# Moving the output projection of a time-mix block behind its FFN, and two early splits of W1

## The chip, the core and the metric

The kernel runs on one core of one Trainium2 chip. The metric is the time of one execution on the device, in microseconds. Before the change it is 949.51 us, the median of three runs (948.9 to 949.73). The profiled execution has a span of 947.2 us, and all clock times below are counted from the start of that span.

## What is computed

Input x is [4, 1024, 512] in f32. It is layer-normalised, and two branches start from the normalised rows.

```
xn  = layernorm(x)
xx  = previous row of xn (row 1 for row 0) - xn
k   = (xn + xx * time_mix_k) @ Wk.T          # 704 hidden channels
r   = (xn + xx * time_mix_r) @ Wr.T
state[t] = state[t-1] * exp(-exp(decay)) + relu(k[t])
att = layernorm((state * r) @ Wv.T) * gamma + beta
ffn = f16(gelu(f16(xn) @ W0.T + bias0) as f16 @ W1.T + bias1)     # 2048 channels
out = x + att + ffn
```

The products of the first branch are taken in f32. For the FFN the weights are split into a high and a low part of type f32r, and each is multiplied with an f16 value held as f32r, so a product of the FFN is two matmuls.

## The kernel before the change

The rows are cut into 8 blocks of 512 tokens, and each block has four subtiles of 128 tokens. The program is unrolled. A scheduler turns the written order into one instruction order for each engine; it uses its own estimates, and it may pull an operation that is written later ahead of others where it believes an engine to be idle. [...]

A block goes through these stages on TensorE, in this order:

- `attention` (line 289). The 704 hidden channels are five chunks of 128 and a half chunk of 64. For each full chunk four matmuls make `pk` and four make `pr` (line 313). ScalarE takes relu of `pk` into `rk` (line 298), VectorE runs the recurrence over it (`st`, line 300) and multiplies by `pr` into `g` (line 324). For the half chunk, k and r share one accumulator, `pkr`: k goes to its partitions 0 to 63 and r to 64 to 127 (lines 328 and 329), and the results go to `gh` (line 336).
- `ffn` (line 398). It is a loop over 16 chunks of the 2048 channels. `up(n)` is eight matmuls into `pd` (line 408), a gelu on ScalarE (line 416) and a cast to f32r on VectorE into `d` (line 418). `down(n, s)` is two matmuls into `pe[s]` for each of the four subtiles (line 423). Two `up` stand ahead of the first `down`.
- `attention_out` (line 341) is called from within that loop, at n = 0. That places the output projection `po` behind pd of chunks 0 and 1. It is 20 full matmuls (line 348, the contraction over 128 channels) and 4 with 64 contraction rows (line 358). `residual` (line 362) then normalises each `po` on VectorE (lines 178, 369, 372, 373) and adds x.
- At n = 4 and n = 7 the loop prepares the next block: layernorm, 16 stream transposes into `xnT` (line 199) and the mixes (lines 276 and 278).
- `finish` (line 391) rounds `pe` to f16 and adds it into the output rows.

PSUM is two pools of four banks: `ps_mm` for pk, pr, pkr, pd and po, and `ps_e` for pe (and for the transposes of block 0). Buffers are taken in turn, so a matmul that opens an accumulator waits for the reader of the accumulator four places earlier.

In block 0 the weights are also prepared. `load_w0(g)` (line 128) loads a quarter of W0 in four pieces and splits each: a copy on ScalarE (line 119) and a subtraction on VectorE (line 120). `load_w1(0, n)` (line 135) does the same with one chunk of W1 and writes both parts to DRAM (line 149), from where later blocks read them (line 151). The raw pieces of W0 and W1 share three buffers, `raw`, so a load waits for the subtraction that ends the use of the buffer.

Of the kernel before, what the change touches and what calls it, by code (L numbers as in the profile page):

```python
# [8 lines left out]
F16 = mybir.dt.float16  # L9
F32 = mybir.dt.float32  # L10
# [4 lines left out]
P = 128  # L15
# [4 lines left out]
def time_mix_and_gelu_ffn(  # L20
# [26 lines left out]
    nc = tc.nc  # L47
    B, T, C = x.shape
    HID = wkT.shape[1]
    N = w0T.shape[1]  # L50
    TB = 512
# [237 lines left out]
    def attention(i, xk):  # L289


        b, t0 = blocks[i]
        g = one.tile([P, NF, TB], F32, tag="g", name=f"g_{i}")
        gh = one.tile([P, NS // 2, P], F32, tag="gh", name=f"gh_{i}")

        def states(h, hw, pk):
            rk = two.tile([P, TB], F32, tag="rk", name=f"rk_{i}_{h}", bufs=1)
            nc.scalar.activation(rk[:hw], pk, AF.Relu)  # L298
            st = two.tile([P, TB], F32, tag="st", name=f"st_{i}_{h}")
            nc.vector.tensor_tensor_scan(  # L300
                st[:hw],
                w_sb[:hw, h : h + 1].to_broadcast([hw, TB]),
                rk[:hw],
                0.0 if t0 == 0 else carry[:hw, h : h + 1],
                ALU.mult,
                ALU.add,
            )
            if t0 + TB < T:
                nc.gpsimd.tensor_copy(carry[:hw, h : h + 1], st[:hw, TB - 1 : TB])
            return st  # L310

        def product(dst, w, cols, src, c):
            nc.tensor.matmul(dst, w[c][:, cols], src, start=(c == 0), stop=(c == NC - 1))  # L313

        for h in range(NF):
            cols = slice(h * P, (h + 1) * P)
            pk = ps_mm.tile([P, TB], F32, tag="mm", name=f"pk_{i}_{h}")
            for c in range(NC):
                product(pk, wk_sb, cols, xk[:, c, :], c)
            st = states(h, P, pk)  # L320
            pr = ps_mm.tile([P, TB], F32, tag="mm", name=f"pr_{i}_{h}")
            for c in range(NC):
                product(pr, wr_sb, cols, xnT[:, c, 1:], c)
            nc.vector.tensor_mul(g[:, h, :], st, pr)  # L324

        both = ps_mm.tile([P, TB], F32, tag="mm", name=f"pkr_{i}")
        for c in range(NC):
            product(both[:HF], wk_sb, slice(H0, HID), xk[:, c, :], c)
            product(both[HF:], wr_sb, slice(H0, HID), xnT[:, c, 1:], c)
        st = states(NF, HF, both[:HF])  # L330

        def tokens(ap, odd):
            return ap.rearrange("p (s two t) -> p s two t", two=2, t=P)[:, :, odd, :]

        for odd in range(2):
            nc.vector.tensor_mul(
                gh[odd * HF : (odd + 1) * HF], tokens(st[:HF], odd), tokens(both[HF:], odd)
            )
        return g, gh

    def attention_out(i, g, gh):

        b, t0 = blocks[i]
        pos = [ps_mm.tile([P, C], F32, tag="mm", name=f"po_{i}_{s}") for s in range(NS)]

        def full(s, first):
            for h in range(NF):
                nc.tensor.matmul(  # L348
                    pos[s],
                    g[:, h, s * P : (s + 1) * P],  # L350
                    wv_sb[:, h, :],
                    start=(first and h == 0),
                    stop=(not first and h == NF - 1),
                )

        def half(s, first):
            rows = slice(s % 2 * HF, (s % 2 + 1) * HF)
            nc.tensor.matmul(  # L358
                pos[s], gh[rows, s // 2, :], wv_sb[rows, NF, :], start=first, stop=not first
            )  # L360

        def residual(s):
            xr = two.tile([P, C], F32, tag="xres", name=f"xres_{i}_{s}")
            nc.sync.dma_start(xr, x[b, t0 + s * P : t0 + (s + 1) * P, :])
            mv = four.tile([P, 1, 2], F32, tag="mv1", name=f"mvy_{i}_{s}")
            stats_of(mv, 0, pos[s], f"sty_{i}_{s}")
            rstd = rstd_of(mv[:, :, 1], f"ry_{i}_{s}")
            z = four.tile([P, C], F32, tag="z", name=f"z_{i}_{s}")
            nc.vector.scalar_tensor_tensor(
                z, pos[s], mv[:, 0, 0:1], gamma_sb, ALU.subtract, ALU.mult  # L370
            )
            nc.vector.scalar_tensor_tensor(z, z, rstd, beta_sb, ALU.mult, ALU.add)
            nc.vector.tensor_add(z, z, xr)
            return z

        early, late = range(NS // 2), range(NS // 2, NS)
        for s in early:
            full(s, True)  # L380
        for s in early:
            half(s, False)
        for s in late:
            half(s, True)
        zs = [residual(s) for s in early]
        for s in late:
            full(s, False)
        zs += [residual(s) for s in late]
        return zs

    def finish(i, s, z, pe):
        b, t0 = blocks[i]
        e16 = two.tile([P, C], F16, tag="e16", name=f"e16_{i}_{s}")
        nc.vector.tensor_add(e16, pe, b1_sb)  # L394
        nc.vector.tensor_add(z, z, e16)  # L395
        nc.sync.dma_start(out[b, t0 + s * P : t0 + (s + 1) * P, :], z)

    def ffn(i, xf, between, state):


        pe = [ps_e.tile([P, C], F32, tag="pe", name=f"pe_{i}_{s}") for s in range(NS)]

        def up(n):
            pd = ps_mm.tile([P, TB], F32, tag="mm", name=f"pd_{i}_{n}")
            cols = slice(n * P, (n + 1) * P)
            for c in range(NC):
                for w in (w0h, w0l):
                    nc.tensor.matmul(  # L408
                        pd,
                        w[c][:, cols],  # L410
                        xf[:, c, :],
                        start=(c == 0 and w is w0h),
                        stop=(c == NC - 1 and w is w0l),
                    )
            d16 = two.tile([P, TB], F16, tag="d16", name=f"d16_{i}_{n}")
            nc.scalar.activation(d16, pd, AF.Gelu, bias=b0_sb[:, n : n + 1])  # L416
            d = wide.tile([P, TB], F32R, tag="d", name=f"d_{i}_{n}", bufs=4)
            nc.vector.tensor_copy(d, d16)  # L418
            return d

        def down(n, s, d, w1):
            for part in range(2):
                nc.tensor.matmul(  # L423
                    pe[s],
                    d[:, s * P : (s + 1) * P],
                    w1[part],
                    start=(n == 0 and part == 0),
                    stop=(n == NN - 1 and part == 1),
                )

        last = 3 if i == len(blocks) - 1 else 0
        AHEAD = 2
        waiting = [(up(n), load_w1(i, n)) for n in range(AHEAD)]
        for n in range(NN):
            if n in between:
                between[n]()
            if n + AHEAD < NN:
                waiting.append((up(n + AHEAD), load_w1(i, n + AHEAD)))  # L440
            if n < NN - last:
                operands = waiting.pop(0)
                for s in range(NS):
                    down(n, s, *operands)
        if last:
            with tc.manual_schedule(engines={nc.tensor.engine, nc.vector.engine}):
                for s in range(NS):
                    for n, operands in zip(range(NN - last, NN), waiting):
                        down(n, s, *operands)
                    finish(i, s, state["zs"][s], pe[s])  # L450
        return pe

    behind = ExitStack()
# [2 lines left out]
    nc.scalar.activation(w_sb, w_sb, AF.Exp)  # L456
    nc.scalar.activation(w_sb, w_sb, AF.Exp, scale=-1.0)
    xf = ffn_input(0, x16s)
    for i in range(len(blocks)):
        more = i + 1 < len(blocks)  # L460
        state = {}
        gs = attention(i, xk)
        if i == 0:
            for grp in range(N // W0G):
                load_w0(grp)
            behind.close()
            load_late_constants()
# [1 line left out]
            x_now = load_x(i + 1)  # L469

        def out_stage():
            state["zs"] = attention_out(i, *gs)

        def next_norm():
            layernorm(i + 1, x_now)
# [2 lines left out]
            transposed(x_now)  # L478
            state["mixed"] = mixed_inputs(i + 1)

        between = {0: out_stage}
        if more:
            between[4] = next_norm
            between[7] = next_inputs
        pe = ffn(i, xf, between, state)
        if more:
            x16s, xk = state["mixed"]
            xf = ffn_input(i + 1, x16s)
            for s in range(NS):
                finish(i, s, state["zs"][s], pe[s])  # L490


# [41 lines left out]
```

## Time and profile before

| What | Value |
|---|---|
| Time, median of 3 | 949.51 us |
| Span of the profiled run, granted TensorE clock | 947.2 us, 0.997 |
| PE busy | 931.0 us (98%) |
| VectorE busy | 485.7 us (51%) |
| ScalarE busy | 160.5 us (17%) |
| pd and pe matmuls (lines 408, 423), records | 1024 and 1024 |
| pk, pr, full po matmuls (lines 313, 348), records | 320 each |
| pkr and half po matmuls, records | 128 and 64 |
| Moved from and to HBM | 89.14 and 16.78 MB |

The page puts 98% of the span on TensorE, but matmul ends are modelled, so lengths below are taken as distances between starts. An f32 matmul appears as two records. In the chain of waits every row is a stretch of the work that ended last; "x8" counts records.

### The profile page before, as it was taken

How to read it: one execution, taken by the hardware profiler on the slowest of the kernel's cores; microseconds unless marked ns; L12 is line 12 of the kernel's file. 1: busy time of each engine (PE TensorE's matmuls, PEld its weight loads, DVE VectorE, ACT ScalarE, POOL GpSimd, SP SyncE). 2: the span in 40 equal slices, each digit the busy share in tenths (PEclk: the TensorE clock that was granted, in tenths of full speed). 3: DMA queues.
4: the chain of work that ended last, by engine and by line, in shares of the span. 5: the costliest groups of instructions: out<-in, count | busy, mean ns of one | idle time of the engine just before them, and what ended most of it. 6: DMA issues, size and time to landing. Idle time of an engine off the chain costs nothing.

```text
span 947.2 us, 8658 instructions
## 1 busy us (share of the span) xinstructions
PE 931.0 (98%) x3216; PEld 583.0 (62%) x3216; DVE 485.7 (51%) x836; ACT 160.5 (17%) x264; POOL 53.7 (6%) x128
## 2 busy tenths in 40 slices
PE   5999999999999999999999999999999999999998
PEld 2447764478644785448854488545884458744686
DVE  6558852385424844259443593436924269232513
ACT  5322321012100121002201022010210102111021
POOL 1011000010001000011000100001000020000100
PEclk9999999999999999999999999999999999999999
DMA  8734570045400354004540155301542024410243
GB/s 271 240 133 145 209 268 1 0 134 199 157 0 21 136 186 148 0 24 142 190 134 1 33 165 180 111 1 57 184 161 88 0 80 143 160 62 0 69 153 111
DMA packets 43368, 106.47 MB, mean 112 GB/s; under 512 B 8256, under 2 KB 8256, under 8 KB 43328
## 3 DMA queue, kind: packets, MB, share of 16 engines
q1 hardware_dynamic: 43328, 105.94, 33.4%
q8 instruction: 25, 0.41, 0.2%
q14 instruction: 15, 0.12, 0.0%
HBM read 89.14 MB, written 16.78 MB: 112 GB/s over the span
## 4 chain that ended last, share of the span: by engine, by line
PE 93%; DVE 4%; ACT 1%; issue 1%; DMA 0%; POOL 0%; DVEq 0%
PE pd L408 23%; PE pe L423 22%; PE po L348 15%; PE pr L313 15%; PE pk L313 14%; PE pkr L313 3%; PE po L358 2%; DVE xnT L199 1%; DVE w L120 1%; DVE stx L178 0%; DVE d L418 0%; DMA x<-in_L_attn_x 0%; DVE z L395 0%; DVE e L394 0%; DVE xk L278 0%
## 5 line engine op out<-in xcount | busy, mean ns | idle before, releaser
L423 PE MATMUL pe<-w,d 128*128 128x512 f32 x1024 | 251.2, 390 | 1.4 <-DVE w L120 0.8
L423 PEld LDWEIGHTS pe<-w,d 128*128 128x128 f32 x1024 | 192.2, 188 | 42.4 <-DVE d L418 1.5
L408 PE MATMUL pd<-xf,w0h 128*128 128x512 f32 x512 | 203.8, 398 | 0.0
L408 PE MATMUL pd<-xf,w0l 128*128 128x512 f32 x512 | 199.9, 390 | 0.0
L416 ACT ACTIVATE d<-pd,b_sb 128x512 f16<-128x512 f32 x128 | 87.9, 686 | 418.2 <-PE pd L408 399.2
L313 PE MATMUL pk<-xk,wk 128*128 128x512 f32 x320 | 145.9, 599 | 3.1 <-DVE xk L245 3.1
L313 PE MATMUL pr<-xnT,wr 128*128 128x512 f32 x320 | 144.0, 592 | 0.0
L348 PE MATMUL po<-wv_sb,g 128*128 128x512 f32 x320 | 140.8, 595 | 0.0
L418 DVE CAST d<-d 128x512 fp32r<-128x512 f16 x128 | 54.1, 424 | 130.7 <-ACT d L416 129.7
L408 PEld LDWEIGHTS pd<-xf,w0h 128*128 128x128 f32 x512 | 96.2, 188 | 28.0 <-issue 5.7
L408 PEld LDWEIGHTS pd<-xf,w0l 128*128 128x128 f32 x512 | 96.2, 188 | 21.6 <-issue 1.9
L313 PEld LDWEIGHTS pk<-xk,wk 128*128 128x128 f32 x320 | 61.0, 192 | 78.3 <-issue 70.9
L313 PEld LDWEIGHTS pr<-xnT,wr 128*128 128x128 f32 x320 | 60.7, 190 | 76.8 <-issue 76.1
L348 PEld LDWEIGHTS po<-wv_sb,g 128*128 128x128 f32 x320 | 60.2, 190 | 75.5 <-issue 74.8
L199 DVE STREAM_TRANSPOSE xnT<-x 32x512 f32<-32x512 f32 x112 | 78.7, 703 | 2.2
L300 DVE TENSOR_TENSOR_SCAN st<-w_sb,carry,rk 128x512 f32<-128x512 f32 (+1 forms) x24 | 30.8, 1282 | 70.2 <-ACT rk L298 70.2
L298 ACT ACTIVATE rk<-pk 128x512 f32<-128x512 f32 x40 | 24.0, 600 | 232.9 <-PE pk L313 232.9
L178 DVE BATCH_NORM_STATS2 sty<-po 128x6 f32<-128x512 f32 x32 | 22.1, 690 | 73.4 <-PE po L358 67.9
L300 DVE TENSOR_TENSOR_SCAN st<-w_sb,rk 128x512 f32<-128x512 f32 (+1 forms) x24 | 29.3, 1222 | 53.6 <-ACT rk L298 53.5
L324 DVE TENSOR_TENSOR g<-st,pr 128x512 f32<-128x512 f32 x40 | 27.5, 688 | 53.7 <-PE pr L313 53.6
L172 POOL TENSOR_SCALAR ry<-mvy 128x1 f32<-128x1 f32 x32 | 11.4, 357 | 503.4 <-DVE mvy L179 503.4
L313 PE MATMUL pkr<-xnT,wr 128*64 128x512 f32 x64 | 29.2, 598 | 0.0
(56 smaller groups left out, 439.6 us busy)
## 6 DMA issues: line engine op xcount, KB each, us to landing
w<-w1d SPq DMA_DIRECT2D x111, 512.0 KB, 3.2
x<-in_L_attn_x SPq DMA_DIRECT2D x32, 256.0 KB, 3.4
xres<-in_L_attn_x SPq DMA_DIRECT2D x32, 256.0 KB, 2.7
w1d<-w SPq DMA_DIRECT2D x16, 512.0 KB, 3.0
out<-z SPq DMA_DIRECT2D x32, 256.0 KB, 4.8
w0raw<-in_L_ffn_W SPq DMA_DIRECT2D x16, 256.0 KB, 4.5
w1raw<-in_L_ffn_W SPq DMA_DIRECT2D x16, 256.0 KB, 3.5
wk<-in_L_attn_Wk SPq DMA_DIRECT2D x4, 352.0 KB, 6.0
```

The source lines that it names most:

```text
L178: nc.vector.bn_stats(st6, src)
L199: nc.vector.transpose(dst[i * Q : (i + 1) * Q, :, :, j, :], src[j * Q : (j + 1) * Q, :, :, i, :],)
L298: nc.scalar.activation(rk[:hw], pk, AF.Relu)
L300: nc.vector.tensor_tensor_scan(st[:hw], w_sb[:hw, h : h + 1].to_broadcast([hw, TB]), rk[:hw], 0.0 if t0 == 0 else carry[:hw, h : h + 1], A ...
L313: nc.tensor.matmul(dst, w[c][:, cols], src, start=(c == 0), stop=(c == NC - 1))
L324: nc.vector.tensor_mul(g[:, h, :], st, pr)
L348: nc.tensor.matmul(pos[s], g[:, h, s * P : (s + 1) * P], wv_sb[:, h, :], start=(first and h == 0), stop=(not first and h == NF - 1),)
L358: nc.tensor.matmul(pos[s], gh[rows, s // 2, :], wv_sb[rows, NF, :], start=first, stop=not first)
L408: nc.tensor.matmul(pd, w[c][:, cols], xf[:, c, :], start=(c == 0 and w is w0h), stop=(c == NC - 1 and w is w0l),)
L416: nc.scalar.activation(d16, pd, AF.Gelu, bias=b0_sb[:, n : n + 1])
L418: nc.vector.tensor_copy(d, d16)
L423: nc.tensor.matmul(pe[s], d[:, s * P : (s + 1) * P], w1[part], start=(n == 0 and part == 0), stop=(n == NN - 1 and part == 1),)
```

## The change

Three things change.

- The output projection of blocks 0 to 6 leaves the FFN loop. `attention_out(i)` now runs behind the FFN of block i. Amid it, between the four half matmuls of `po` and the last ten full ones, the half chunk of k and r of block i+1 is computed (`half_chunk`); then the rest of po, and then the five full chunks of block i+1 (`full_chunks`). The last block keeps its projection inside its FFN. The half chunk's accumulator `pkr` moves from `ps_mm` to `ps_e`.
- `finish` is cut in two. `rounded` makes the f16 rows `e16` right after the FFN, which frees `pe`; the buffers for `e16` go from two to four.
- In block 0 the chunks 0 and 1 of W1 are loaded and split behind the first quarter of W0 and ahead of the other three, since the first `down` no longer has the projection of block 0 in front of it.

The core of the diff:

```diff
-        for h in range(NF):
...
-        both = ps_mm.tile([P, TB], F32, tag="mm", name=f"pkr_{i}")
...
+        def full_chunks():
+            g = one.tile([P, NF, TB], F32, tag="g", name=f"g_{i}")
...
+        def half_chunk():
+            gh = one.tile([P, NS // 2, P], F32, tag="gh", name=f"gh_{i}")
+            both = ps_e.tile([P, TB], F32, tag="pe", name=f"pkr_{i}")
...
         for s in late:
             half(s, True)
+        amid()
         zs = [residual(s) for s in early]
...
-        e16 = two.tile([P, C], F16, tag="e16", name=f"e16_{i}_{s}")
+        e16 = four.tile([P, C], F16, tag="e16", name=f"e16_{i}_{s}")
...
         if i == 0:
-            for grp in range(N // W0G):
+            load_w0(0)
+            early = [load_w1(0, n) for n in range(2)]
+            for grp in range(1, N // W0G):
                 load_w0(grp)
...
-        between = {0: out_stage}
-        if more:
-            between[4] = next_norm
-            between[7] = next_inputs
-        pe = ffn(i, xf, between, state)
+        pe = ffn(i, xf, {4: next_norm, 7: next_inputs} if more else {0: out_stage}, state, early)
...
+            e16s = [rounded(i, s, pe[s]) for s in range(NS)]
             xf = ffn_input(i + 1, x16s)
+            full_chunks, half_chunk = attention(i + 1, xk)
+            next_gh = []
+            zs = attention_out(i, g, gh, lambda: next_gh.append(half_chunk()))
+            gh = next_gh[0]
             for s in range(NS):
-                finish(i, s, state["zs"][s], pe[s])
+                finish(i, s, zs[s], e16s[s])
+            g = full_chunks()
```

More of the change, by code (lines that the diff above doesn't have):

```diff
@@ L292, in attention @@
         b, t0 = blocks[i]
-        g = one.tile([P, NF, TB], F32, tag="g", name=f"g_{i}")
-        gh = one.tile([P, NS // 2, P], F32, tag="gh", name=f"gh_{i}")
         def states(h, hw, pk):
@@ L313, in product @@
             nc.tensor.matmul(dst, w[c][:, cols], src, start=(c == 0), stop=(c == NC - 1))
-        for h in range(NF):
[L316 to L324, printed above, removed]
@@ L326, in attention @@
-        both = ps_mm.tile([P, TB], F32, tag="mm", name=f"pkr_{i}")
[L327 to L330, printed above, removed]
+        def full_chunks():
+            g = one.tile([P, NF, TB], F32, tag="g", name=f"g_{i}")
+            for h in range(NF):
+                cols = slice(h * P, (h + 1) * P)
+                pk = ps_mm.tile([P, TB], F32, tag="mm", name=f"pk_{i}_{h}")
+                for c in range(NC):
+                    product(pk, wk_sb, cols, xk[:, c, :], c)
+                st = states(h, P, pk)
+                pr = ps_mm.tile([P, TB], F32, tag="mm", name=f"pr_{i}_{h}")
+                for c in range(NC):
+                    product(pr, wr_sb, cols, xnT[:, c, 1:], c)
+                nc.vector.tensor_mul(g[:, h, :], st, pr)
+            return g
@@ L332, in tokens @@
         def tokens(ap, odd):
             return ap.rearrange("p (s two t) -> p s two t", two=2, t=P)[:, :, odd, :]
[L335 to L341, printed above, removed]
+        def half_chunk():
+            gh = one.tile([P, NS // 2, P], F32, tag="gh", name=f"gh_{i}")
+            both = ps_e.tile([P, TB], F32, tag="pe", name=f"pkr_{i}")
+            for c in range(NC):
+                product(both[:HF], wk_sb, slice(H0, HID), xk[:, c, :], c)
+                product(both[HF:], wr_sb, slice(H0, HID), xnT[:, c, 1:], c)
+            st = states(NF, HF, both[:HF])
+            for odd in range(2):
+                nc.vector.tensor_mul(
+                    gh[odd * HF : (odd + 1) * HF],
+                    tokens(st[:HF], odd),
+                    tokens(both[HF:], odd),
+                )
+            return gh
@@ L343, in attention_out @@
+        return full_chunks, half_chunk
+    def attention_out(i, g, gh, amid=lambda: None):
         b, t0 = blocks[i]
@@ L389, in attention_out, with rounded, finish, ffn @@
         return zs
-    def finish(i, s, z, pe):
+    def rounded(i, s, pe):
+        e16 = four.tile([P, C], F16, tag="e16", name=f"e16_{i}_{s}")
+        nc.vector.tensor_add(e16, pe, b1_sb)
+        return e16
+    def finish(i, s, z, e16):
         b, t0 = blocks[i]
-        e16 = two.tile([P, C], F16, tag="e16", name=f"e16_{i}_{s}")
-        nc.vector.tensor_add(e16, pe, b1_sb)
         nc.vector.tensor_add(z, z, e16)
         nc.sync.dma_start(out[b, t0 + s * P : t0 + (s + 1) * P, :], z)
-    def ffn(i, xf, between, state):
+    def ffn(i, xf, between, state, early=()):
+        early = dict(enumerate(early))
         pe = [ps_e.tile([P, C], F32, tag="pe", name=f"pe_{i}_{s}") for s in range(NS)]
@@ L434, in ffn @@
         AHEAD = 2
-        waiting = [(up(n), load_w1(i, n)) for n in range(AHEAD)]
+        waiting = [(up(n), early.get(n) or load_w1(i, n)) for n in range(AHEAD)]
         for n in range(NN):
@@ L449, in ffn @@
                         down(n, s, *operands)
-                    finish(i, s, state["zs"][s], pe[s])
+                    finish(i, s, state["zs"][s], rounded(i, s, pe[s]))
         return pe
@@ L458, in time_mix_and_gelu_ffn @@
     xf = ffn_input(0, x16s)
+    state = {}
+    full_chunks, half_chunk = attention(0, xk)
+    g = full_chunks()
+    gh = half_chunk()
     for i in range(len(blocks)):
         more = i + 1 < len(blocks)
-        state = {}
-        gs = attention(i, xk)
         if i == 0:
-            for grp in range(N // W0G):
+            load_w0(0)
+            early = [load_w1(0, n) for n in range(2)]
+            for grp in range(1, N // W0G):
                 load_w0(grp)
@@ L471, in out_stage @@
         def out_stage():
-            state["zs"] = attention_out(i, *gs)
+            state["zs"] = attention_out(i, g, gh)
         def next_norm():
@@ L479, in next_inputs @@
             state["mixed"] = mixed_inputs(i + 1)
-        between = {0: out_stage}
-        if more:
-            between[4] = next_norm
-            between[7] = next_inputs
-        pe = ffn(i, xf, between, state)
+        pe = ffn(i, xf, {4: next_norm, 7: next_inputs} if more else {0: out_stage}, state, early)
+        early = ()
         if more:
             x16s, xk = state["mixed"]
+            e16s = [rounded(i, s, pe[s]) for s in range(NS)]
             xf = ffn_input(i + 1, x16s)
+            full_chunks, half_chunk = attention(i + 1, xk)
+            next_gh = []
+            zs = attention_out(i, g, gh, lambda: next_gh.append(half_chunk()))
+            gh = next_gh[0]
             for s in range(NS):
-                finish(i, s, state["zs"][s], pe[s])
+                finish(i, s, zs[s], e16s[s])
+            g = full_chunks()
 _TRANSPOSED = {"L0_attn_Wk", "L0_attn_Wr", "L0_attn_Wv", "L0_ffn_W0", "L0_ffn_W1"}
```

## The prediction

> **What bounds the kernel now.** I read the page first, then the chain of waits in order of time, then the timeline of single engines in three stretches. The page's row of engines and its chain by engine agree on the engine:
>
> ```profile
> PE 931.0 (98%) x3216; PEld 583.0 (62%) x3216; DVE 485.7 (51%) x836; ACT 160.5 (17%) x264; POOL 53.7 (6%) x128
> PE 93%; DVE 4%; ACT 1%; issue 1%; DMA 0%; POOL 0%; DVEq 0%
> ```
>
> TensorE sets the end, and VectorE has half its time free. The chain in order of time (start, length, work) shows what a block is made of; here is block 1 from its last k and r products to its third pd:
>
> ```profile
> 164.12 3.44 PE pr L313 x8
> 167.56 3.59 PE pkr L313 x16
> 171.15 3.90 PE pd L408 x16
> 175.05 8.58 PE po L348 x20
> 183.63 1.92 PE po L358 x8
> 185.54 8.78 PE po L348 x20
> 194.33 1.85 PE pd L408 x8
> ```
>
> There is no gap in it. Block 2 begins at 248.78 and block 3 at 364.34, 115.56 us apart, and all blocks in between repeat that. So per block only the matmuls themselves and the joints between kinds can be shortened. A full f32 record takes 8.58/20 = 0.429 us, an f32r record 1.814/8 = 0.227. Without joints a block is 120 full f32 records, 8 pairs of pkr (16 records, two at a time) and 4 pairs of half po, all at 0.429, and 256 f32r records: 132 x 0.429 + 256 x 0.227 = 114.7 us. The joints cost the other 0.85 us. TensorE's timeline shows them one by one, for instance pkr to pd:
>
> ```profile
> 170.12 0.59 PE L313 MATMUL pkr<-xk,wk 128*64 128x512 f32 x1
> 170.55 0.59 PE L313 MATMUL pkr<-xk,wk 128*64 128x512 f32 x1
> 171.08 0.50 PE L408 MATMUL pd<-xf,w0h 128*128 128x512 f32 x1
> 171.42 0.40 PE L408 MATMUL pd<-xf,w0l 128*128 128x512 f32 x1
> ```
>
> Starts are 0.43 apart inside pkr, then 0.53, then 0.34 where 0.227 is the rule; some 0.06 more goes in the next pd. That joint is 0.27. Read in the same way: pr to pkr 0.14, full po to half po 0.19 (183.04, 183.56, 184.09), half back to full 0.20, po to pd 0.04 and pd to po none. The sum is 0.84.
>
> Block 0 has the only later stop of TensorE, in its FFN (the bracket gives the idle time and its releaser):
>
> ```profile
> 111.95 0.50 PE L423 MATMUL pe<-w,d 128*128 128x512 f32 x1 [0.30 <-DVE d L418]
> 113.21 1.87 PE L423 MATMUL pe<-w,d 128*128 128x512 f32 x7 [0.76 <-DVE w L120]
> ```
>
> [...] every change between full, column-split (pkr) and row-split (half po) costs 0.14 to 0.27. [...] at 113.21 a matmul waits for a split that stood behind other VectorE work. No stop of TensorE above comes from PSUM; [...] I check the buffers that the new order takes in turn.
>
> **The change part by part.**
>
> *Joints.* Per block there were four changes of mode: pr/pkr, pkr/pd, full/half, half/full. Behind the FFN the order is pe, full po, half po, pkr, full po, pk, pr, pd. pe to po is f32r to f32, free like pd to po and pe to pk. Then full/half 0.19; half/pkr, which no trace shows, between 0.14 (pr to pkr) and 0.20 (half to full), I take 0.16; pkr/po 0.20 like half/full; pr to pd 0.04 like po to pd. The sum is 0.59, so 0.25 less. Seven projections move: 7 x 0.25 = **-1.75 us**. If half/pkr were free, it would be 7 x 0.41 = -2.9.
>
> *The projection behind the FFN.* Its g and gh are long written, so it starts at once. Its four banks last held pd 12 to 15, which ScalarE has read. Let T be the start of pk of the next block. The DVE rows of residual in block 1 (184.72 to 192.98 and 194.36 on) give the spacings. The first statistics start 1.16 after the half po starts, at T-12.9; six more operations than before (three adds of e16, the half-chunk scan of 1.28, two products) fit before T: z of subtile 1 ends at T-6.2, gh at T-4.0, z of subtile 2 at about T. Then come po 3, and the next-but-one block's statistics and normalisation, which the scheduler pulled here: st of chunk 0 starts at T+4.8, the four normalisations (0.54 each) end at T+11. Who waits? pr of chunk 1 needs the bank of po 3, read at T+2.6, and starts at T+10.3. pr of chunk 2 needs g of chunk 0, ready at T+8.1, and starts at T+17.2. pr of chunk 3 needs g of chunk 1: bound by pr 1 itself (ends T+13.7), ready at T+14.7, wanted at T+24.0. pk and pr last 3.43 each, so VectorE is ahead everywhere: **0**. Four transposes (0.71 each) then stand ahead of the cast d 0; g 4 ends at T+35.3, so d 0 at T+38.6, and pe 0 starts at T+39.9: **0**. `rounded` does sooner what finish did, hidden as before.
>
> *Block 0, the stop that goes.* With no residual in this FFN, the transposes and mixes are spread over chunks 0 to 7 with w1 splits between them; each cast and split comes 3 us or more ahead of its down: -(0.30 + 0.76) = **-1.05 us**.
>
> *Block 0, the wait that comes.* 19.3 us of po stood ahead of pe 0; now it follows pd 0 to 2 directly. pkr ends at 53.96, pd 0 to 2 take 3.90 + 1.81, so pe 0 is due at 59.67 and needs d 0. In the kernel before, VectorE's list there is:
>
> ```profile
> 53.12 1.22 DVE L300 TENSOR_TENSOR_SCAN st<-w_sb,rk 128x512 f32<-128x512 f32 x1
> 54.44 0.69 DVE L324 TENSOR_TENSOR g<-st,pr 128x512 f32<-128x512 f32 x1
> 55.12 1.22 DVE L300 TENSOR_TENSOR_SCAN st<-w_sb,rk 64x512 f32<-64x512 f32 x1
> 56.44 0.86 DVE L336 TENSOR_TENSOR gh<-st,pkr 64x256 f32<-64x256 f32 x2
> 57.34 0.43 DVE L418 CAST d<-d 128x512 fp32r<-128x512 f16 x1
> ```
>
> In the built program of the changed kernel five stream transposes of block 1 stand within this list: one ahead of the half-chunk scan, one behind it, three behind gh; d 0, d 1 and all the rest of TensorE's work wait behind them. The transposes overwrite xnT, so the first waits for pkr too.
>
> ```profile
> L199 DVE STREAM_TRANSPOSE xnT<-x 32x512 f32<-32x512 f32 x112 | 78.7, 703 | 2.2
> ```
>
> Lower bound: from 54.15 (pkr done), 5 x 0.71 + 1.25 + 0.86 + 0.43 = 6.1, d 0 at 60.3, a wait of 0.7. The other bound is the weights. Ahead of st of chunk 4 stand all 16 splits of W0, and two of W1, where it was 16 and two as well, in another order (the last of these 18 ended at 51.0). New are the two writes of W1 to DRAM in the middle (1 MB; the DMA engines are 0.6 to 0.8 busy from 28 to 44), block 1's statistics and normalisations (4 x 0.68, 4 x 0.18, 4 x 0.54 = 5.6 us) between the splits, and a buffer's next load that waits for each split. Following the three raw buffers with loads of 3.0 us puts the last split at 51.7 and d 0 at 60.5; with loads of 4.5 us, as most were between 33 and 44, at 54.0 and 62.7. So the wait is 0.7 to 3.1, I take **+2.0 us**.
>
> Sum: 949.5 - 1.75 - 1.05 + 2.0 = **948.7 us**, 0.8 less, not to be told from no change.
>
> **The rivals.** *The early transposes cost their least* and the half/pkr joint is cheap: 949.5 - 1.75 to -2.9 - 1.05 + 0.7 = 946.3 to 947.4, faster. For it: VectorE idles some 12 us between 23 and 48 in the kernel before, room for the new work. Against it: that idle time is waiting for loads, and the loads wait for splits.
> *W0 comes late.* If the writes and the in-order statistics cost the chain of loads 3 us more than my slow case, the wait is 6: 949.5 - 1.75 - 1.05 + 6 = 952.7, slower. For it: every microsecond there is one of TensorE's. Against it: only 18 loads, and 30% of the DMA time is free.
> *VectorE becomes the bound behind the FFN.* It works without a break from T-12.9 to T+11. If it were late by 0.5 us in six blocks: +3.0, 951.7. Against it: every wait that I checked has 1.3 us or more to spare, most have 7.
>
> **How the numbers follow.** My forecast 0.57, the cheap case 0.28, late W0 0.10, VectorE 0.05. The forecast with waits of 1.0 to 3.1 spans 947.7 to 949.8. The range is 946.8 to 951.3: it takes in most of the cheap case and the near end of the last two. Faster by over 0.2% (below 947.6) 0.29, within 0.2% 0.57, slower (above 951.4) 0.14.
>
> **What would show it.** Right: blocks 1 to 6 about 115.3 us apart and without a gap; one mode change fewer; pe 0 of block 0 stopped by DVE d for about 2 us near 60, with five transposes ahead of that cast; no stop near 112. Wrong: a gap at pr or pk in blocks 1 to 6 with VectorE as releaser; a half/pkr joint above 0.4 us; the wait at pe 0 released by a split of W0 or above 4 us.

## The result and the profile after

The changed kernel takes 953.9 us (median of six executions, 952.09 to 954.68) against 949.66 us before on the same chip. The ratio is 1.0043, with a 95% interval of 1.003 to 1.0056: it is 4.2 us slower. The prediction was 948.7, with a range up to 951.3. The profiled execution has a span of 952.6 us.

The page's row of engines and the chain by engine, as before. The busy time of TensorE (the PE row) rose by only 1.6 us, and TensorE sets the end in even more of the span:

```profile
PE 932.6 (98%) x3216; PEld 585.6 (61%) x3216; DVE 486.4 (51%) x836; ACT 161.0 (17%) x264; POOL 56.5 (6%) x128
PE 97%; DVE 2%; DMA 0%; ACT 0%; issue 0%; SPq 0%
```

The chain of waits in order of time (start, length, work) at the seam of blocks 0 and 1 shows the new order, full po, half po, pkr, full po, pk, without a gap:

```profile
121.09 8.58 PE po L356 x20
129.68 1.92 PE po L366 x8
131.59 3.59 PE pkr L312 x16
135.18 8.78 PE po L356 x20
143.96 3.43 PE pk L312 x8
```

The projections of the next blocks start at 236.39, 351.69 and so on to 812.89: six distances of 115.30 us, where blocks were 115.56 apart before. Steady state is thus faster, as predicted, and the loss must lie ahead of 121.09. TensorE's timeline there has one stop. The bracket is the idle time and its releaser; VectorE's timeline below it shows what stood ahead of the cast `d` that released it:

```profile
65.74 3.75 PE L438 MATMUL pe<-w,d 128*128 128x512 f32 x8 [4.86 <-DVE d L433]
```

```profile
56.76 0.69 DVE L120 TENSOR_TENSOR w0l<-w0raw,w0h 128x512 fp32r<-128x512 f32 x1 [0.22 <-ACT w0h L119]
57.37 1.22 DVE L299 TENSOR_TENSOR_SCAN st<-w_sb,rk 128x512 f32<-128x512 f32 x1
58.51 0.67 DVE L120 TENSOR_TENSOR w<-w1raw,w 128x512 fp32r<-128x512 f32 x1
...
59.69 0.69 DVE L199 STREAM_TRANSPOSE xnT<-x 32x512 f32<-32x512 f32 x1
...
61.52 0.70 DVE L199 STREAM_TRANSPOSE xnT<-x 32x512 f32<-32x512 f32 x1
...
63.01 2.13 DVE L199 STREAM_TRANSPOSE xnT<-x 32x512 f32<-32x512 f32 x3
65.17 0.76 DVE L433 CAST d<-d 128x512 fp32r<-128x512 f16 x2
```

To be seen are the five stream transposes, as the prediction named them, and above them the last split of W0 at 56.76. It ends at 57.4, where the prediction's slowest case had 54.0. The input of `d` had been there for some time. ScalarE's timeline has the gelus of chunks 0 and 1 in one row:

```profile
60.59 1.26 ACT L431 ACTIVATE d<-pd,b_sb 128x512 f16<-128x512 f32 x2
```

The first of them ended by 61.3 (one takes 0.69), and the cast started 3.9 us later, after the operations that stood ahead of it in VectorE's list. pd of chunk 0 starts at 55.13 and three pd take 5.58 (that is their distance where nothing stops them, below), so pe 0 was due at 60.71 and came 5.03 late.

There is a second loss in the same place. From the first pe to the next pd it took 3.55 us, where 1.81 is the rule, and the records of that pd stand 0.43 us apart (69.29, 69.72, 70.15), where 0.23 is the rule. The windows of the changed kernel (from and to, length, then busy time of PE, weight loads, VectorE, ScalarE and GpSimd with counts, granted clock of TensorE, DMA share, GB/s):

```profile
64.00:66.00 2.00, 0.26 (x1) 0.29 (x2) 1.93 (x5) 0.31 (x1) 0.00 (x0) 0.57 0.00 0
66.00:68.00 2.00, 2.00 (x5) 1.53 (x5) 1.92 (x4) 0.38 (x1) 0.00 (x0) 0.50 0.00 0
68.00:70.00 2.00, 2.00 (x6) 1.60 (x5) 1.97 (x3) 0.47 (x1) 0.00 (x0) 0.50 0.00 0
70.00:72.00 2.00, 2.00 (x8) 1.54 (x8) 1.77 (x3) 0.15 (x1) 0.00 (x0) 0.73 0.15 59
```

The clock column reads 0.57, 0.50, 0.50, 0.73. What is missing to 1, times 2 us, sums to 0.86 + 1.00 + 1.00 + 0.54 = 3.40 us, or half the clock for 6.8 us. Of these 6.8 TensorE was still idle for 1.5, so the half clock cost (6.8 - 1.5)/2 = 2.7 us.

The stop near 112 us of before is gone; no bracket follows the pe in this place:

```profile
111.86 1.98 PE L438 MATMUL pe<-w,d 128*128 128x512 f32 x8
```

It had been longer than its brackets (0.30 + 0.76). By starts, the pe due at 111.48 was followed by a pd at 114.91, which is 3.43 for work of 1.81: a stop of 1.62.

The balance from the end of pkr of block 0, which sets apart that this execution reached it 1.24 us later: 952.6 - 55.20 = 897.4 against 947.2 - 53.96 = 893.2, so 4.2 more. The terms give 5.03 + 2.7 - 1.62 - 7 x 0.265 (joints, from the distances of blocks) = 4.3.

What was open: why d 0 was 3 us later than the forecast, whether the half clock follows from the stop, and whether the early splits of W1 were to blame or the move of the projection. In all that follows, "stop" is the start of pe 0, less that of pd 0, less 5.58. It depends on two things: when d 0 is ready, and when TensorE gets to pd 0. The second is between 53.9 and 55.4 us in the profiles (53.89 in the kernel before, 55.13 in the changed one), and with an early pd 0 the same d 0 makes a longer stop.

### The profile page after: what moved, and what is told of

The parts are those of the page before. It is cut to its first block, busy times and chain, and to the rows that moved or that the text cites. A ratio compares the mean times of both kernels' runs of the same rounds, so it can differ in the third digit from the quotient of the medians.

```text
span 952.6 us, 8633 instructions
## 1 busy us (share of the span) xinstructions
PE 932.6 (98%) x3216; PEld 585.6 (61%) x3216; DVE 486.4 (51%) x836; ACT 161.0 (17%) x264; POOL 56.5 (6%) x128
## 4 chain that ended last, share of the span: by engine, by line
PE 97%; DVE 2%; DMA 0%; ACT 0%; issue 0%; SPq 0%
PE pd L423 24%; PE pe L438 24%; PE pk L312 15%; PE po L356 15%; PE pr L312 14%; PE pkr L312 3%; PE po L366 2%; DMA x<-in_L_attn_x 0%; PE pt L226 0%; DVE xnT L199 0%; DVE z L408 0%; DVE e L403 0%; DVE stx L178 0%; DVE st L299 0%; DVE d L433 0%
```

## The experiments

**The transposes.** The changed kernel, with block 1's transposes and mixes held behind the cast d 0. The statistics and normalisation stay where they were. `tc.issue_after` puts what is issued within it behind the named instruction in the list of its engine.

```diff
+    def after_cast(i, n):
+        return tc.issue_after(casts[i, n].ins) if i == 0 else ExitStack()
...
-            transposed(x_now)
-            state["mixed"] = mixed_inputs(i + 1)
+            with after_cast(i, 0):
+                transposed(x_now)
+                state["mixed"] = mixed_inputs(i + 1)
```

> The changed kernel with one edit: block 1's stream transposes and mixes stand behind the cast d 0 of block 0 in VectorE's list; block 1's statistics and normalisation stay early. Theory (VectorE's list): five transposes, 3.6 us, leave the list ahead of d 0, so pe 0 waits 4.9 - 3.6 = 1.3 us, and a wait that short no longer lowers TensorE's clock, which gives back another 2.6 us; the kernel takes 953.9 - 3.6 - 2.6 = 947.7, below the kernel before. If the clock is not tied to the length of the wait: 953.9 - 3.6 = 950.3. Rival (the new order of the projection costs by itself, the list of block 0 does not matter): 953.5 or more.

Measured: 948.5 us (21 executions, ratio to before 0.9991, 0.9984 to 0.9997), 5.4 less than the changed kernel. The profiled execution took 947.6, the expected time; the median is 0.8 above it.

```profile
61.15 2.09 PE L438 MATMUL pe<-w,d 128*128 128x512 f32 x8 [1.03 <-DVE d L433]
```

The stop is 1.19, 3.8 less, of which the five transposes of 0.70 are 3.5, and the first pe takes 2.09 us, with 1.00 in the clock column from 54 to 74. The new place of the projection is not what costs.

**The normalisation.** As above, and block 1's layernorm behind d 0 too.

```diff
-            layernorm(i + 1, x_now)
+            with after_cast(i, 0):
+                layernorm(i + 1, x_now)
```

> The changed kernel with block 1's layernorm held behind d 0 as well, so that nothing of block 1 stands on VectorE ahead of d 0 of block 0. Theory: the last splits of W0 no longer wait for normalisations, 0.5 to 1.2 us each, the buffers come free and the loads start sooner; d 0 comes 1 to 2 us earlier than with the transposes held alone, the wait of pe 0 is 0 to 0.5 us, and the kernel takes 946.2 to 946.8. Rival (the two writes of W1 alone delay the loads, the normalisations fill time that VectorE waits in anyway): the same as with the transposes held alone, 947.7.

Measured: 947.99 us (13 executions, 0.9984, 0.9976 to 0.9993). The stop falls to 0.45, so the early normalisation cost d 0 another 0.7, less than the 1 to 2 expected. The time falls by only 0.5: with all of block 1's work now between 60 and 94, a split of W1 comes late there and stops a pe near 94. From pe 0 to the next po it is 53.37 us instead of 52.70, so that stop is 0.7. The expected 946.2 to 946.8 was missed for these two reasons.

**The writes, behind W0.** The changed kernel, with the two writes of W1's first chunks to DRAM (1 MB) issued behind the last load of W0.

```diff
-            nc.sync.dma_start(w1_dram[n].bitcast(F32), w1.bitcast(F32))
+            if held is None:
+                nc.sync.dma_start(w1_dram[n].bitcast(F32), w1.bitcast(F32))
+            else:
+                held.append((n, w1))
...
+            with tc.issue_after(last_raw.ins):
+                for n, w1 in held:
+                    nc.sync.dma_start(w1_dram[n].bitcast(F32), w1.bitcast(F32))
```

> The changed kernel with one edit: the two writes of W1's first chunks to DRAM (1 MB) are issued behind the last load of W0. VectorE's order is left to the scheduler. Theory (the writes are one of several causes): the loads behind them land 1 to 2 us sooner, pe 0 waits 3 to 4 us instead of 4.9, the clock still drops in part; 951.5 to 953. Rival (the loads are all that delays d 0): the wait falls to about 2 us as predicted for the changed kernel, the clock stays, 948.5 to 949.5. Rival (only VectorE's list matters): 953.5 to 954.

Measured: 952.81 us (five executions, 1.0032, 1.0019 to 1.0045). The stop is 4.78, hardly shorter, and the clock was at half for 6.8 us again (0.80, 0.50, 0.50, 0.50 and 0.99 in the five windows from 62 to 72). In this trace the last split of W0 ends at 54.3, 0.1 ahead of pd 0, where it ended 2.3 behind pd 0 in the changed kernel. But the load of W1's chunk 2 was now the one behind the writes: issued at 50.57, it landed 4.93 later, and its split (56.18) stands ahead of the scan of chunk 4 in VectorE's list. The writes had been moved from one place of the row to another.

**The writes, behind the whole row.** The same writes behind the load of chunk 2, the last of the 19 raw loads (16 of W0, three of W1) whose splits stand ahead of d 0 in VectorE's list. Early splits and five transposes stay.

```diff
+            held.append((n, w1))
+            if n >= 2:
+                with tc.issue_after(load.ins):
+                    for m, part in held:
+                        nc.sync.dma_start(w1_dram[m].bitcast(F32), part.bitcast(F32))
+                held.clear()
```

> The changed kernel with the writes of W1's chunks 0 and 1 issued behind the load of chunk 2, the last of the 19 raw loads that the scan of chunk 4 stands behind on VectorE; W1's early splits and the five transposes stay. Theory (the place of the 1 MB of writes within the row of raw loads is what the early splits cost; their order against W0 is not): d 0 comes as in the kernel with the projection alone, some 3 us sooner, pe 0 waits 1.4 to 2 us, and the kernel takes 950.4. Rival (the early splits delay W0 by their own two loads): 952.8, as with the writes directly behind W0. Rival (writes do not matter anywhere): 953.9.

Measured: 950.31 us (13 executions, 1.0002, 0.9994 to 1.001), 3.6 less than the changed kernel, as the theory said. The stop is 2.71, longer than the 1.4 to 2 expected, since TensorE was at pd 0 as early as 54.26. The scan of chunk 4 starts at 54.57, 0.3 behind pd 0; in the changed kernel it started at 57.37, 2.2 behind, and the split of chunk 2 came behind it, at 58.51. d 0 starts at 61.98 instead of 65.17.

**The projection alone.** W1's chunks 0 and 1 split behind all of W0, as before the change.

```diff
-            load_w0(0)
-            early = [load_w1(0, n) for n in range(2)]
-            for grp in range(1, N // W0G):
+            early = ()
+            for grp in range(N // W0G):
```

> The projection behind the FFN alone: W1's first two chunks are split behind all of W0, as before the change. In VectorE's list the same 16 splits of W0 and three of W1 stand ahead of the scan of chunk 4, but only three stream transposes (not five) ahead of d 0, and no writes of W1 amid the loads of W0. Theory (the list decides, whatever order the weights have): d 0 comes 1.4 us sooner for the transposes and some 0.3 for the writes, so pe 0 waits 3.0 to 3.5 us instead of 4.9, [...] 950 to 952.4. Rival (the early splits are needed, without them pe 0 waits for W1): a wait of 6 us or more released by a split of W1, 955 or more.

Measured: 950.41 us (13 executions, 1.0002, 0.9994 to 1.001).

```profile
62.53 2.08 PE L438 MATMUL pe<-w,d 128*128 128x512 f32 x8 [1.43 <-DVE d L433]
```

The releaser is d 0, not a split of W1: the early splits that the change added for pe 0 are not needed. The expectation had the time right but not the way to it: the trace shows five transposes ahead of d 0 here as well, not three, and the stop is 1.60, not 3.0 to 3.5. With the same five transposes as the changed kernel, the gain comes from the raw loads, whose writes again follow the whole row. The run before kept the early splits and has the same time, and d 0 at 61.98, where it is at 61.95 here; its longer stop is pd 0, 1.1 us earlier there. Together this settles what the early splits cost: 3.5 us, and through their writes.

**The early splits alone**, in the kernel before.

```diff
-            for grp in range(N // W0G):
+            load_w0(0)
+            early = [load_w1(0, n) for n in range(2)]
+            for grp in range(1, N // W0G):
...
-        pe = ffn(i, xf, between, state)
+        pe = ffn(i, xf, between, state, early)
```

> The kernel before with the other part of the change alone: W1's chunks 0 and 1 split ahead of three quarters of W0, the projection left inside the FFN. Theory: pe 0 has 19 us of po in front of it, so a later end of W0's splits costs nothing there; pd 0 needs only the first quarter of W0. The same as before, 949.8 (949.3 to 950.3). Rival (the early splits delay work that TensorE waits for in block 0 whatever the order): 951 or more, with a stop at pd or pe released by a split of W0.

Measured: 950.04 us (13 executions, 1.0002, 0.9994 to 1.0011), no difference, and the same stop of a pe with the brackets 0.29 and 0.77. With 19 us of po ahead of pe 0, late weights are hidden. Neither part alone makes the kernel slower; the loss needs both.

**The clock, first try.** The changed kernel with the first three transposes left ahead of d 0.

```diff
+                with ExitStack() if j * (P // Q) + i < free else hold():
                     nc.vector.transpose(
...
-            transposed(x_now)
+            transposed(x_now, 3, lambda: after_cast(i, 0))
```

> The changed kernel with all of block 1's transposes but the first three, and the mixes, behind the cast d 0: three instead of five stand ahead of it. A wait of about 1.03 + 3 x 0.70 = 3.1 us at pe 0, between the 1.03 with the clock at full speed and the 4.6 to 4.9 with the clock at half. Theory [...]: full clock, 953.9 - 1.8 - 2.6 = 949.5. Rival (the loss grows with the stop): about half of the 2.6 us is lost as well, 950.8. Rival (any stop above 2 us costs the whole): 952.1.

Measured: 952.2 us (eight executions, 1.0024, 1.0014 to 1.0035). The stop came out at 3.71, longer than the 3.1 meant, and the clock was at half for 3.4 us (0.72, 0.50 and 0.92 in the three windows from 62 to 68). The theory was about a stop of 3.1, so with this one it is not decided.

**The clock, second try.** Two transposes.

```diff
-            transposed(x_now, 3, lambda: after_cast(i, 0))
+            transposed(x_now, 2, lambda: after_cast(i, 0))
```

> The changed kernel with two stream transposes ahead of the cast d 0. With three the stop was 3.54 us and the clock fell. A stop of about 3.54 - 0.7 = 2.8 us. Theory [...]: clock at full in the profile, and a time of 952.2 - 0.7 less most of the loss, 949.5 to 950. Rival (a stop above 2 us is enough): clock at half for some us in the profile, 951.5.

Measured: 951.08 us (nine executions, 1.0024, 1.0011 to 1.0037), nearer to the rival's 951.5 than to the theory's 949.5 to 950. The stop is 2.28, and yet the windows of this kernel and, after them, of the kernel with the writes behind the whole row (stop 2.71) read:

```profile
62.00:64.00 2.00, 1.26 (x5) 1.11 (x6) 1.88 (x5) 0.69 (x1) 0.00 (x0) 0.95 0.02 6
64.00:66.00 2.00, 2.00 (x6) 1.53 (x6) 1.92 (x4) 0.36 (x1) 0.00 (x0) 0.50 0.00 0
66.00:68.00 2.00, 2.00 (x8) 1.59 (x7) 1.94 (x4) 0.26 (x1) 0.00 (x0) 0.70 0.00 0
```

```profile
62.00:64.00 2.00, 1.45 (x4) 1.20 (x5) 1.96 (x4) 0.69 (x1) 0.00 (x0) 0.59 0.00 0
64.00:66.00 2.00, 2.00 (x7) 1.59 (x6) 1.92 (x4) 0.00 (x0) 0.00 (x0) 0.56 0.00 0
```

Missing to 1, times 2 us: 0.10 + 1.00 + 0.60 = 1.70 and 0.82 + 0.88 = 1.70. The theory, which expected a full clock with a stop of about 2.8 us, falls: the clock was at half for 3.4 us with 2.28 as well as with 2.71.

**Both holds, and the writes behind W0.** The edits of the normalisation and of the writes behind W0 together.

```diff
+            with after_cast(i, 0):
+                layernorm(i + 1, x_now)
...
+            with tc.issue_after(last_raw.ins):
```

> Both edits: nothing of block 1 ahead of d 0 on VectorE, and the two writes of W1 behind the last load of W0. Theory: no wait of pe 0 is left, and only the joints (1.8 us less) and the stop near 112 (1.6 us less) remain: 949.7 - 1.8 - 1.6 = 946.3, provided that the held work does not bring a new stop later in block 0; each such stop adds its length. If the wait cannot be brought under 1 us by either: 947.3 or more. Rival (the order behind the FFN costs by itself): 950 or more.

Measured: 947.57 us (nine executions, 0.9976, 0.9967 to 0.9986). pe 0 has no stop at all. Of the 1.2 us above the expectation, the stop near 94 (bracket 0.38 on a split of W1) is again about 0.7 by starts. In the profiled execution the rest is a late start: TensorE was at pd 0 at 55.36, 0.8 later than in the fastest kernel below (54.58).

**The mixes spread.** As that, with each of the four groups of mixes behind a later cast, so that they stand singly between the splits of W1.

```diff
+        def next_mixes():
+            state["mixed"] = mixed_inputs(i + 1, lambda c: after_cast(i, 8 + c))
...
+        if i == 0:
+            between[10] = next_mixes
```

> The version meant to beat both: block 1's layernorm and transposes behind d 0, the writes of W1's first chunks behind the last load of W0, and the four groups of mixes behind the casts of chunks 8, 9, 10 and 11, so that they stand singly between the splits of W1. Theory: the stops at pe near 94 us (0.7 to 0.8 by starts, released by a split of W1 that stood behind a row of mixes) go as well; 947.57 - 0.8 = 946.8. Rival (those stops are not what the last microsecond is): 947.4 or more.

Measured: 946.8 us (five executions, 0.9968, 0.9956 to 0.9981), as expected. The stop near 94 is gone. pe 0 still has a stop of 0.84, because TensorE was at pd 0 as early as 53.91; d 0 starts at 59.76.

**The same without the early splits of W1.** The writes then follow the row of loads by themselves.

```diff
-            load_w0(0)
-            held = []
-            early = [load_w1(0, n, held) for n in range(2)]
+            early = ()
```

> The projection behind the FFN without the early splits of W1, with block 1's layernorm and transposes behind d 0 and the mixes behind the casts of chunks 8 to 11. Theory (the early splits are not needed, and cost time): d 0 comes before pd 2 ends, no stop of pe 0 is left, and the kernel takes 946.1 to 946.8, at most that of the version with early splits (946.8). Rival (pe 0 then waits for the split of W1's chunk 0): a stop there released by a split of W1, 948 or more.

Measured: 946.5 us (five executions, 946.32 to 946.58; 0.9967, 0.9954 to 0.9979), the fastest kernel here, 3.2 us below the kernel before. The chain of waits:

```profile
54.66 5.66 PE pd L424 x24
60.32 1.81 PE pe L439 x8
```

Three pd and then pe 0 without a stop; by starts 54.58 and 60.16, the 5.58 used above. d 0 starts at 57.60, 2.2 earlier than with the early splits.

**The kernel before, mixes spread.** The projection stays inside the FFN, and the groups of mixes stand behind the casts of chunks 9 to 12.

```diff
+            state["mixed"] = mixed_inputs(i + 1, lambda c: after_cast(i, 9 + c))
```

> The kernel before, projection inside the FFN, with one edit: block 1's mixes stand behind the casts of chunks 9 to 12 in block 0, singly between the splits of W1. Theory (the stop near 112 us is a matter of VectorE's list, not of where the projection stands): the stop of 1.5 us goes, 949.75 - 1.5 = 948.2; the distance from here to the best version with the projection moved is the joints, 1.8 us. Rival (the stop only moves to a later chunk, or the mixes come late for block 1): 949.3 or more.

Measured: 948.35 us (21 executions, 0.9985, 0.9978 to 0.9991). The stop near 112 goes without the projection being moved. From here to the best version, 948.35 - 946.5 = 1.85 us, is what the move is worth when nothing of block 0 stands against it.

**All together.** A stop and a piece of half clock are read from one execution, so they are set against the span of that execution, not against a median. The span worked out is that of the fastest kernel's profile (944.4), plus the stops, plus half of the time that TensorE worked at half clock, plus what pd 0 started later than 54.58.

| Kernel | pd 0 at, us | Stops, us | Worked at half clock, us | Span worked out | Span of the profile |
|---|---|---|---|---|---|
| Fastest (spread, no early splits) | 54.58 | 0 | 0 | 944.4 | 944.4 |
| Mixes spread | 53.91 | 0.84 | 0 | 944.6 | 944.7 |
| Both holds, writes behind W0 | 55.36 | 0 and 0.7 | 0 | 945.9 | 945.9 |
| Normalisation held | 54.33 | 0.45 and 0.7 | 0 | 945.3 | 945.4 |
| Transposes held | 54.38 | 1.19 | 0 | 945.4 | 945.5 |
| Projection alone | 55.35 | 1.60 | 0 | 946.8 | 946.9 |
| Two transposes early | 54.88 | 2.28 | 3.4 | 948.7 | 948.7 |
| Writes behind the row | 54.26 | 2.71 | 3.2 | 948.4 | 948.4 |
| Three transposes early | 54.03 | 3.71 | 3.0 | 949.0 | 949.1 |
| Writes behind W0 | 54.41 | 4.78 | 5.3 | 951.6 | 951.5 |
| Changed kernel | 55.13 | 5.03 | 5.3 | 952.6 | 952.6 |

The second figure of a stop is the one near 94. All eleven agree within 0.1 us: from pe 0 to the end these kernels take the same 884.2 us, but for the half clock and the stop near 94. Nothing larger is left to explain in these executions.

The medians hold other executions too. The 13 of the projection alone fall in two groups, five from 948.1 to 949.0 with a mean clock of 0.999 to 1.000 and eight from 950.1 to 951.5 with 0.995 to 0.998; the profile is of the first. Traces of the second were not taken, so what makes them slower is not shown.

## Why the prediction was wrong, step by step

*Joints*: right. 1.75 us forecast; 7 x 0.265 = 1.86 by the distances of blocks and 1.85 by the two kernels with mixes spread. The chain shows three changes between full, half-po and pkr matmuls in a block, where there were four. The joint from half po to pkr, which no trace had shown, is far below the 0.4 us that would have overturned the step. Starts are 0.52 and 0.48 apart where 0.43 is the rule, so it is 0.14, forecast 0.16:

```profile
361.60 0.59 PE L366 MATMUL po<-wv_sb,gh 64*128 64x512 f32 x2
362.12 0.64 PE L312 MATMUL pkr<-xk,wk 128*64 128x512 f32 x1
...
362.60 0.59 PE L312 MATMUL pkr<-xk,wk 128*64 128x512 f32 x1
```

*The projection behind the FFN*, put at 0: right. No gap in blocks 1 to 6, and the rival in which VectorE becomes the bound there is ruled out.

*The stop that goes*: right, and worth 1.62 instead of 1.05, since the brackets show less than the distances of starts. It was not a merit of the move, as the kernel before with spread mixes shows.

*"Block 0, the wait that comes"*: the step that failed. Put at +2.0 with bounds of 0.7 to 3.1, it was 5.03 + 2.7 = 7.7. Two terms were wrong.

The first is the end of the splits of W0. The slow bound let the last one end at 54.0, together with pkr; it ended at 57.4, 2.3 behind pd 0. The prediction also misread the kernel before: there the scan of chunk 4 (53.12) stood behind 16 splits of W0 and three of W1, the third at 52.51, and not behind 18 that ended at 51.0. The prediction had the two writes in its list of what is new, but it put their effect into loads of 3.0 to 4.5 us. In the trace the raw load issued right behind the writes, at 31.38, reached ScalarE only at 37.26, 5.9 us later. With three buffers each load also waits for a split (SyncE's queue stood 9.7 us in nine such waits at line 132, the longest 3.5), so the delay travels down the row. Moving the writes behind the row gave back 2.3 us of stop (d 0 came 3.2 us earlier), holding the transposes 3.8, and holding the normalisation on top of that 0.7. These are effects of removals one at a time, and they overlap. The transposes' own cost was as worked out (3.5 against 3.6), and from the end of the last split of W0 to the end of d 0 it took 8.2 us, where the prediction's two cases have 8.8 and 8.7.

The second is the clock, in no step at all. Neither the forecast with its stop of 2.0 us nor the rival with a stop of 6 us counted it. The profiles show the loss with the stops of 2.28, 2.71, 3.71, 4.78 and 5.03 us, and none with those of 0.45 to 1.60. In the changed kernel this second price of the stop was 2.7 us.

*The rivals*: "W0 comes late" is what happened, at a chance of 0.10. Its 952.7 counted a stop of 6 without the clock; the stop was 5.0, and the clock added 2.7. "The early transposes cost their least" is ruled out in the changed kernel, and describes rather the versions that hold them. Of the signs that the prediction named as showing it wrong, the one that came was a wait at pe 0 above 4 us.

## What to carry to other kernels

When a change takes away work that stood in front of a consumer, the whole chain behind that consumer has to be costed with its buffers: here the raw loads, in which 1 MB of writes put in the middle cost 3.5 us, and which were hidden as long as 19 us of po stood ahead. On an engine that works off a list, as VectorE did when the cast `d` started 3.9 us after its input was there, hold the next block's work behind the operation that the bound engine waits for, and spread it between later ones; that made a slower kernel into the fastest. Read the clock column behind every stop of TensorE: here stops of 2.28 to 5.03 us were followed by 3.4 or 6.8 us at half clock, and so cost more than their length.

## What the runs showed of the hardware

Every row is one profiled execution, read at pe 0 of block 0. The clock column is given from its first window below 1.00 to its last, in windows of 2 us ("throughout" is from 54 to 74); the time at half clock is twice what is missing to 1, times 2 us.

| Kernel | Stop, us | Clock column | At half clock, us |
|---|---|---|---|
| Normalisation held | 0.45 | 1.00 throughout | 0 |
| Mixes spread | 0.84 | 1.00 throughout | 0 |
| Transposes held | 1.19 | 1.00 throughout | 0 |
| Projection alone | 1.60 | 1.00 throughout | 0 |
| Two transposes early | 2.28 | 0.95, 0.50, 0.70 | 3.4 |
| Writes behind the row | 2.71 | 0.59, 0.56 | 3.4 |
| Three transposes early | 3.71 | 0.72, 0.50, 0.92 | 3.4 |
| Writes behind W0 | 4.78 | 0.80, 0.50, 0.50, 0.50, 0.99 | 6.8 |
| Changed kernel | 5.03 | 0.57, 0.50, 0.50, 0.73 | 6.8 |

What brings a fall on and what sets its length was not shown. One also stands elsewhere: the kernel before has one of 3.4 us early in block 0 (0.88, 0.50 and 0.77 in the three windows from 12 to 18), where the changed kernel reads 1.00 throughout.

The executions of the kernel with the writes behind the row lie in two groups: five from 948.3 to 948.7 us with a mean clock of 0.998 to 1.000, and eight from 950.0 to 951.8 with 0.995 to 0.998. Only one of them was traced, so it is not shown that a fall at pe 0 makes the difference. The mean clock also counts a fall elsewhere: 3.4 us at half clock in 948.4 us make 0.998 by themselves.
